# Four layers of a convolution network in float32: the attention heads of the first image's first layer, written as a pinned pipeline over key blocks

## The chip, the cores and the metric

The kernel runs on one core of one Trainium2 chip, in float32 throughout. The metric is the device time of one whole call in microseconds (us), which is the time from the first to the last instruction of all four images. The time before the change is the median of three runs.

## The reference, cut to what matters

Four residual layers are applied to four images of 32 x 32 positions and 384 channels. The change touches only the first layer, and only for the first image. That layer is an attention with six heads of 64 channels, deformed sampling positions, and a bias that is interpolated from a table for each pair of query and key:

```python
q = einsum('bhwc,cd->bhwd', x, w_q) + b_q
# a grouped 3x3 convolution of q, layer norm, gelu and tanh give pos, the sampling positions
xs = _bilinear_sample(xg, pos)
k = (xs @ w_k + b_k).reshape(Bq, n, HEADS, HC)
v = (xs @ w_v + b_v).reshape(Bq, n, HEADS, HC)
attn = einsum('bmhc,bnhc->bhmn', qh, k) * scale
bias = _bilinear_sample(rpe_img, disp)         # disp: from every query to every pos
attn = softmax(attn + bias, axis=-1)
out = einsum('bhmn,bnhc->bmhc', attn, v)
return out @ w_out + b_out                      # x + this goes to layers 1, 2 and 3
```

Here n is 1024, so each head has 1024 queries by 1024 keys. Layers 1 to 3 (a second attention, a box filter and a neighbourhood attention) are not touched.

## The kernel before, in words

Two lanes produce the instructions. The class `Front` computes layer 0 and the class `Trunk` computes layers 1, 2 and 3. Each lane takes its SBUF buffers from its own side: `Front` from the right, `Trunk` from the left (L90, the pools of `scope`, L293 to L298). `Net.layer0` (L257) runs the front of image 0 to its end before anything else is written down. After that `Net.layer3` (L271) writes the trunk of image b and mixes in the fronts of images 1 to 3, so that a front stays a tenth of an image ahead of the trunk (`TRUNK_STEPS`, `FRONT_STEPS`, `LEAD`, L62). So the front of image 0 stands alone, and the trunk of image 0 cannot begin before it, because it reads `x1`, which is that front's result.

Within each engine's queue the framework decides at build time, by its own estimate, which instruction comes next; the order of the program is only a priority. An instruction that is passed to `keep_in_program_order` (called `pin` in the code) is fixed behind everything that was written before it on its engine. Each engine works off its queue in order. A buffer tag with `bufs=k` has k places, and a new tile waits until the last reader of the place is done.

`Front.layer0` (L402) has three stages. `inputs0` (L518) makes the padded queries `qpad`, the sampling positions, the indices `widx` and weights `bias_f` of the bias, then the keys `k0` (L707, in DRAM) and the values `va` (L712). The heads stage (scope "l0b", L416 to L424) runs over 6 heads `h`, 2 halves `q` of 512 queries, and in `head0` (L719) over 8 blocks `j` of 128 keys, which makes 96 blocks in 12 halves. The last stage (L425 to L434) is the output projection.

For one block, `head0` does this. GpSimd gathers a window of the bias table (`win`, L734). ScalarE scales its upper rows into `z` (L746) and VectorE adds the scaled lower rows (L747). ScalarE scales the left columns into `lg` (L751) and VectorE adds the scaled right columns (L752). TensorE multiplies keys by queries (L755), VectorE adds the product to `lg` (L756) and takes the running maximum (L759, L761). After eight blocks the maximum is brought to all partitions: four transposes on TensorE (L768), a reduction on VectorE (`top`, L772), a diagonal on GpSimd (`diag`, L774), a product with ones on TensorE (L776), a copy on ScalarE (`tb`, L780). Only then each of the eight blocks has `tb` subtracted (L787, VectorE), is exponentiated (L788, ScalarE) and goes into two products, with the values and with ones for the row sums (L790). Two copies (L794, L797) and a DMA (L798) save the half. After each pair of heads `over_sums` (L801) loads the row sums through DRAM, takes the reciprocal (L808), sends it through DRAM again (L811, L816) and multiplies `qpad` by it (L821).

In `head0` nothing is pinned. The buffers of the heads stage lie in the place on the right side that `inputs0` used before: 4 places for `win`, 3 for `z`, 13 for `lg`.

## Time and profile before

| what | value |
|---|---|
| median of three runs | 4876.06 us (4868.23 to 4881.34) |
| the profiled execution's own time | 4831.1 us |
| its span from the first to the last instruction | 4829.3 us |
| mean granted TensorE clock | 0.91 of full speed |
| TensorE busy | 4189.8 us, 87% of the span |
| VectorE busy | 3132.9 us, 65% |
| ScalarE busy | 2404.9 us, 50% |
| GpSimd busy | 946.3 us, 20% |

The profile is one execution on the chip. Busy time is the time in which an engine worked on at least one instruction. A group of the profile shows one line of the code on one engine, with the count, the mean duration of one in nanoseconds, and the idle time of the engine just before these instructions with what ended it ("<-"). The table of stretches shows, for each stretch of time, its length, then for each engine the busy us and in brackets the number of instructions, then the granted TensorE clock, the busy share of the DMA engines and their GB/s. Instructions of one engine are pipelined, so the next can start before the one before has ended; a duration is therefore a little longer than the distance between two starts.

In the profiled execution the last instruction of the value projection (L712) of image 0 starts at 221.78 us, the heads stage follows, and its last running maximum ends at 599.7 us.

### The profile page before, as it was taken

What the parts mean: (1) busy time and instruction counts of PE and PEld (TensorE: products, weight loads), DVE (VectorE), ACT (ScalarE), POOL (GpSimd) and SP (SyncE); (2) the same over time, 40 slices, a digit from 0 to 9 for tenths busy, and PEclk for the clock granted to TensorE, in tenths of its full rate; (3) what the DMA queues carried; (4) which work ended last, traced back from release to release, by engine and by line L of the source; (5) the groups of instructions that cost most, each with busy time, mean ns of one, the idle gap of its engine ahead of it and who ended that gap; (6) DMA issues with size and microseconds to landing.
All of it is one profiled execution on the core that took longest, in us unless ns stands there. A gap on an engine that the chain in (4) does not pass through costs nothing.

```text
span 4829.3 us, 46659 instructions
## 1 busy us (share of the span) xinstructions
PE 4189.8 (87%) x15704; PEld 1799.4 (37%) x15704; DVE 3132.9 (65%) x5727; ACT 2404.9 (50%) x3693; POOL 946.3 (20%) x946
## 2 busy tenths in 40 slices
PE   5466678899999989889999989899999998999998
PEld 2222233333333353333333444343333335343444
DVE  3478828676877836577777762767687873454544
ACT  2155414565766513376666532457576641456642
POOL 1533303211212101421211210422121210000000
PEclk7677788999999989899999989799999998899998
DMA  6323244311212143431221224532121213201011
GB/s 118 102 84 92 70 131 144 94 53 38 80 50 73 36 147 105 126 86 50 60 62 54 65 76 113 154 92 56 33 80 42 75 45 114 87 23 33 19 39 40
DMA packets 230927, 366.82 MB, mean 76 GB/s; under 512 B 117475, under 2 KB 164672, under 8 KB 230688
## 3 DMA queue, kind: packets, MB, share of 16 engines
q1 hardware_dynamic: 169672, 197.36, 14.0%
q0 software_dynamic: 39936, 145.53, 10.3%
q10 hardware_dynamic: 21080, 20.96, 1.8%
q8 instruction: 124, 2.03, 0.2%
q14 instruction: 115, 0.94, 0.1%
HBM read 285.84 MB, written 78.21 MB: 75 GB/s over the span
## 4 chain that ended last, share of the span: by engine, by line
PE 35%; ACT 9%; DVE 7%; issue 3%; DMA 2%; POOL 0%; SPq 0%; ACTq 0%; DVEq 0%; POOLq 0%
PE bank L1184 8%; PE big L1154 4%; PE big L376 3%; PE big L1035 3%; PE bank L790 3%; PE bank L390 2%; PE bank L755 2%; PE bank L1128 2%; ACT big L1044 2%; PE bank L1179 2%; DVE e L1193 1%; DVE nmax L1043 1%; ACT e L1162 1%; PE big L1074 1%; PE bank L1472 1%
## 5 line engine op out<-in xcount | busy, mean ns | idle before, releaser
L1193 DVE SCALAR_TENSOR_TENSOR e<-bank,gam,e 128x512 f32<-128x512 f32 x768 | 557.6, 748 | 564.9 <-ACT gn L1192 275.1
L1184 PE MATMUL bank<-sim,sg 128*128 128x512 f32 (+3 forms) x2304 | 870.6, 512 | 2.8 <-DVE e L1193 2.8
L1044 ACT ACTIVATE big<-big,nmax 128x1024 f32<-128x1024 f32 x384 | 418.5, 1090 | 384.5 <-DVE nmax L1043 384.0
L734 POOL DMA_INDIRECT win<-strips,widx x384 | 425.8, 1109 | 887.4 <-DVE z L747 450.3
L1162 ACT ACTIVATE e<-big 128x1024 f32<-128x1024 f32 x384 | 376.8, 1019 | 360.2 <-PE big L1154 355.0
L1184 PEld LDWEIGHTS bank<-sim,sg 128*128 128x128 f32 x2304 | 405.9, 199 | 378.1 <-issue 297.7
L1043 DVE TENSOR_REDUCE nmax<-big 128x1 f32<-128x1024 f32 x384 | 453.1, 1217 | 54.4 <-PE big L1035 53.0
L1154 PE MATMUL big<-qa,ka 64*128 64x512 f32 x1536 | 412.1, 627 | 15.5 <-ACT big L1044 9.4
L1139 POOL TENSOR_SCALAR sg<-sim,gam 128x512 f32<-128x512 f32 x192 | 147.3, 770 | 1416.5 <-PE bank L1184 1126.9
L1035 PE MATMUL big<-k,q 32*128 32x512 f32 x1536 | 357.6, 701 | 74.5 <-ACT e L1162 37.0
L790 PE MATMUL bank<-lg,va 128*64 128x512 f32 x768 | 374.1, 634 | 44.7 <-ACT lg L788 44.6
L755 PE MATMUL bank<-qpad,kz 128*128 128x512 f32 x768 | 375.8, 620 | 22.6 <-DVE e L1193 13.7
L790 PE MATMUL bank<-lg,ones 128*64 128x512 f32 x768 | 373.4, 634 | 0.0
L746 ACT ACTIVATE z<-win,bias_f 128x528 f32<-128x528 f32 x384 | 277.0, 737 | 188.8 <-DVE lg L752 108.6
L752 DVE SCALAR_TENSOR_TENSOR lg<-z,bias_f,lg 128x512 f32<-128x512 f32 x384 | 299.9, 795 | 45.5 <-ACT lg L751 43.9
L747 DVE SCALAR_TENSOR_TENSOR z<-win,bias_f,z 128x528 f32<-128x528 f32 x384 | 291.8, 779 | 38.5 <-ACT z L746 38.1
L652 POOL DMA_INDIRECT gat<-pairs,sidx x192 | 210.8, 1098 | 448.1 <-DVE ix_gt L464 244.5
L751 ACT ACTIVATE lg<-z,bias_f 128x512 f32<-128x512 f32 x384 | 267.5, 719 | 44.1 <-DVE z L747 27.2
L787 DVE TENSOR_TENSOR lg<-lg,tb 128x512 f32<-128x512 f32 x384 | 246.2, 698 | 64.7 <-ACT tb L780 64.7
L756 DVE TENSOR_TENSOR lg<-bank,lg 128x512 f32<-128x512 f32 x384 | 256.3, 683 | 32.0 <-PE bank L755 30.7
L788 ACT ACTIVATE lg<-lg 128x512 f32<-128x512 f32 x384 | 222.4, 629 | 40.2 <-DVE lg L787 39.8
L1154 PEld LDWEIGHTS big<-qa,ka 64*128 64x128 f32 x1536 | 134.7, 188 | 272.0 <-issue 156.8
(262 smaller groups left out, 5812.2 us busy)
## 6 DMA issues: line engine op xcount, KB each, us to landing
pairs<-xn SPq DMA_DIRECT2D x64, 192.0 KB
q<-qd SPq DMA_DIRECT2D x48, 256.0 KB
w<-in_gmat SPq DMA_DIRECT2D x16, 576.0 KB
w<-in_w_off SPq DMA_DIRECT2D x12, 576.0 KB
w<-in_Wqkv SPq DMA_DIRECT2D x12, 576.0 KB
a<-in_x SPq DMA_DIRECT2D x16, 384.0 KB
x<-a ACTq DMA_DIRECT2D x4, 1536.0 KB
k<-a SPq DMA_DIRECT2D x12, 512.0 KB
```

Source lines behind the costliest of these rows:

```text
L734: nc.gpsimd.indirect_dma_start(out=win, out_offset=None, in_=self.strips[:, :], in_offset=bass.IndirectOffsetOnAxis(ap=self.widx[:, q, c : ...
L747: v.scalar_tensor_tensor(z, wv[:, 1 : HH + 1, 0 : HW + 1], sc(0, 1), z, ALU.mult, ALU.add)
L752: v.scalar_tensor_tensor(lg, z[:, :, 1 : HW + 1], sc(0, 0), lg, ALU.mult, ALU.add)
L755: nc.tensor.matmul(ps, kz[:, j * P : (j + 1) * P], both, start=True, stop=True)
L790: nc.tensor.matmul(po[out, :], w, lf, start=j == 0, stop=j == NJ - 1)
L1035: nc.tensor.matmul(ps[r][:, h * 512 : (h + 1) * 512], self.q4[rows, i * P : (i + 1) * P], self.k4[rows, 0:512], start=True, stop=True,)
L1043: v.tensor_reduce(nmax[:, r, i : i + 1], ps[r], AX.X, ALU.max, negate=True)
L1044: nc.scalar.activation(ps[r], ps[r], AF.Exp, bias=nmax[:, r, i : i + 1], accum_out=den[:, r, i : i + 1],)
L1154: nc.tensor.matmul(ps[:, r, :], ka[rows, j * P : (j + 1) * P], qa[rows, cols], start=True, stop=True,)
L1162: nc.scalar.activation(e, ps, AF.Exp)
L1184: nc.tensor.matmul(ps[:, (mid - i0) * P :], sg[:, r, m, :], sim[:, r, m, mid * P : i1 * P], start=m == 0, stop=m == 1,)
L1193: v.scalar_tensor_tensor(e[:, r, :], ps, self.gam[:, 1:2], e[:, r, :], ALU.add, ALU.mult, accum_out=tot[:, r, h : h + 1],)
```

## The change

Only image 0 is changed; images 1 to 3 still use `head0`. The heads of image 0 are now written by a new generator `heads0`. It has one sequence of 96 blocks across all heads and halves, and in each turn `t` it does one step of each phase for different blocks: the window gather for block t+13, the two bias steps on VectorE for blocks t+8 and t+7, the two on ScalarE for t+8 and t+9, the key products for t+2 and t+3 (every second turn, into one two-bank tile), the addition and the running maximum for block t, the subtraction and the exponential for block t-10, the two value products for block t-11. The steps of the maximum follow at the turn of a half, and `divide` does the work of `over_sums` in three steps, 0, 4 and 9 turns after the pair's last block was saved. All compute instructions are pinned; DMAs and gathers are not. The buffers are on the left side, with 8 places for `win`, 5 for `z` and 23 for `lg`. The generator is started inside `inputs0`, ahead of the key and value projections, where it writes turns -9 to -4; the rest follows after `inputs0`. The output projection is moved unchanged into `outputs0`.

```diff
@@ -411,6 +411,17 @@
             self.va = self.wt([P, NJ, C], "va")
             self.f = self.wt([P, 2, 2, NJ * G], "bias_f")
             self.widx = self.wt([P, 2, NJ * G], "widx", 1, I32)
+            if b == 0:
+                self.side = "left"
+                with self.scope("l0f"):
+                    self.side = "right"
+                    self.heads = self.heads0(self.work)
+                    with self.scope("l0a"):
+                        yield from self.inputs0(b)
+                    yield from self.heads
+                yield from self.outputs0(b)
+                return
             with self.scope("l0a"):
                 yield from self.inputs0(b)
             with self.scope("l0b"):
@@ -422,16 +433,20 @@
                         yield from self.head0(h, q)
                     if h % 2:
                         yield from self.over_sums(h // 2)
-            with self.scope("l0c"):
-                w = self.weights("w_out")
-                for ko in range(KC):
-                    rows = slice(ko * P, (ko + 1) * P)
-                    x = self.wt([P, N], "res", 2)
-                    nc.sync.dma_start(x, self.x0[b % 2][rows, :])
-                    ps = self.dense_t(w, self.qpad, ko)
-                    v.scalar_tensor_tensor(x, ps, self.col(C_BOUT, ko), x, ALU.add, ALU.add)
-                    nc.sync.dma_start(self.x1[b % 2][rows, :], x)
-                    yield 6
+            yield from self.outputs0(b)
+    def outputs0(self, b):
+        nc, v = self.nc, self.nc.vector
+        with self.scope("l0c"):
+            w = self.weights("w_out")
+            for ko in range(KC):
+                rows = slice(ko * P, (ko + 1) * P)
+                x = self.wt([P, N], "res", 2)
+                nc.sync.dma_start(x, self.x0[b % 2][rows, :])
+                ps = self.dense_t(w, self.qpad, ko)
+                v.scalar_tensor_tensor(x, ps, self.col(C_BOUT, ko), x, ALU.add, ALU.add)
+                nc.sync.dma_start(self.x1[b % 2][rows, :], x)
+                yield 6
 
     def positions(self, oall):
 
@@ -698,6 +713,9 @@
                 xss[j] = weigh(j, gats.pop(j))
             if j > 0:
                 yield 7
+        if b == 0:
+            next(self.heads)
         va = self.va
         kT = self.wt([P, KC, N], "a12", 2)
         w = self.weights("w_k")
@@ -797,6 +815,199 @@
         nc.scalar.copy(den, po[o0 : o0 + 1, :])
         nc.sync.dma_start(self.den[h][:, q * HN : (q + 1) * HN], den)
         yield 3
+    def heads0(self, work):
+        nc, v, pin = self.nc, self.nc.vector, self.tc.keep_in_program_order
+        f, va = self.f, self.va
+        HH, HN = HW // 2, N // 2
+        NI = HN // P
+        blocks = [(h, q, j) for h in range(G) for q in range(2) for j in range(NJ)]
+        n = len(blocks)
+        AHEAD, SUB, OUT = 8, 10, 11
+        win, z, lg, ps, half, dens, inv = {}, {}, {}, {}, {}, {}, {}
...
+        def divide(step, k):
+            heads = (2 * k, 2 * k + 1)
...
+            if step == 0:
+                dens[k] = tile_of([P, 2, NJ], "dens", 2)
+                for r, h in enumerate(heads):
+                    nc.sync.dma_start(dens[k][:, r, :], by_row(self.den[h]))
+            elif step == 1:
+                pin(v.reciprocal(dens[k], dens[k]))
+                for r, h in enumerate(heads):
+                    nc.sync.dma_start(by_row(self.rden[h]), dens[k][:, r, :])
+                for q in range(2):
+                    inv[q] = tile_of([P, HN], "lg", 23)
+                    for r, h in enumerate(heads):
+                        nc.sync.dma_start(
+                            inv[q][r * GC : (r + 1) * GC],
+                            self.rden[h][0, q * HN : (q + 1) * HN].partition_broadcast(GC),
+                        )
+            else:
+                for q in range(2):
+                    out = queries(2 * k, q)
+                    w = inv[q].rearrange("p (y x) -> p y x", x=HW)
+                    pin(v.tensor_tensor(out, out, w, ALU.mult))
+        def turn(t):
+            i = t + AHEAD
+            if i + 5 < n:
+                h, q, j = blocks[i + 5]
+                win[i + 5] = tile_of([P, (HH + 1) * WROW], "win", 8)
...
+            at = lambda i: blocks[i][2] * G + blocks[i][0]
+            sc = lambda i, axis, side: f[:, side, axis, at(i) : at(i) + 1]
+            if 0 <= i < n:
+                wv = win.pop(i).rearrange("p (r c) -> p r c", c=WROW)
+                pin(v.scalar_tensor_tensor(
+                    z[i], wv[:, 1 : HH + 1, 0 : HW + 1], sc(i, 1, 0), z[i], ALU.mult, ALU.add
+                ))
+            if 0 <= i - 1 < n:
+                zi, lf = z.pop(i - 1), lg[i - 1].rearrange("p (y x) -> p y x", x=HW)
+                pin(v.scalar_tensor_tensor(
+                    lf, zi[:, :, 1 : HW + 1], sc(i - 1, 0, 0), lf, ALU.mult, ALU.add
+                ))
+            if 0 <= i < n:
+                lg[i] = tile_of([P, HN], "lg", 23)
+                pin(nc.scalar.activation(
+                    lg[i].rearrange("p (y x) -> p y x", x=HW),
+                    z[i][:, :, 0:HW],
+                    AF.Copy,
+                    scale=sc(i, 0, 1),
+                ))
+            if 0 <= i + 1 < n:
+                wv = win[i + 1].rearrange("p (r c) -> p r c", c=WROW)
+                z[i + 1] = tile_of([P, HH, HW + 1], "z", 5)
+                pin(nc.scalar.activation(
+                    z[i + 1], wv[:, 0:HH, 0 : HW + 1], AF.Copy, scale=sc(i + 1, 1, 1)
+                ))
+            if t >= -2 and (t + 2) % 16 == 0 and t + 18 < n and t + 2 >= 16:
+                self.load_keys(blocks[t + 18][0])
+            if t >= -2 and t % 2 == 0 and t + 2 < n:
+                big = self.big()
+                for u in range(2):
+                    h, q, j = blocks[t + 2 + u]
+                    ps[t + 2 + u] = big[:, u * 512 : (u + 1) * 512]
+                    pin(nc.tensor.matmul(
+                        ps[t + 2 + u],
+                        self.kz[h % 2][:, j * P : (j + 1) * P],
+                        queries(h, q),
+                        start=True,
+                        stop=True,
+                    ))
+            m = (t - 1) // NJ
+            if t > 0 and t % NJ == 0 and t <= n:
+                top = tile_of([P, NI], "top", 2)
+                pin(v.tensor_reduce(
+                    top, half[m, "t"].rearrange("p (i n) -> p i n", i=NI), AX.X, ALU.max
+                ))
+                diag = tile_of([P, NI, P], "diag", 1)
+                pin(nc.gpsimd.tensor_tensor(
+                    diag, bc(self.ident, 1, NI), bc(top, 2, P), ALU.mult
+                ))
+            if 0 <= t < n:
+                m, j = divmod(t, NJ)
+                pin(v.tensor_tensor(lg[t], ps.pop(t), lg[t], ALU.add))
+                if j == 0:
+                    half[m] = tile_of([P, HN], "rmax", 2)
+                else:
+                    first = lg[t - 1] if j == 1 else half[m]
+                    pin(v.tensor_tensor(half[m], first, lg[t], ALU.max))
+                if j == NJ - 1:
+                    half[m, "t"] = self.bank()
+                    for i in range(NI):
+                        cols = slice(i * P, (i + 1) * P)
+                        pin(nc.tensor.transpose(half[m, "t"][:, cols], half[m][:, cols], self.ident))
+            if t > 1 and t % NJ == 1 and t <= n + 1:
+                m = (t - 2) // NJ
+                half[m, "b"] = tile_of([P, HN], "tb", 2)
+                pin(nc.scalar.copy(half[m, "b"], half[m, "p"]))
+            s = t - SUB
+            if 0 <= s < n:
+                tb = half[s // NJ, "b"]
+                pin(v.tensor_tensor(lg[s], lg[s], tb, ALU.subtract))
+                pin(nc.scalar.activation(lg[s], lg[s], AF.Exp))
+            o = t - OUT
+            if 0 <= o < n:
+                h, q, j = blocks[o]
+                if j == 0:
+                    half[o // NJ, "o"] = self.bank()
+                po = half[o // NJ, "o"]
+                for own, w in ((True, va[:, j, h * GC : (h + 1) * GC]), (False, self.ones[:, 0:GC])):
+                    pin(nc.tensor.matmul(
+                        po[rows(h, own), :], w, lg[o], start=j == 0, stop=j == NJ - 1
+                    ))
+            if t > 0 and t % NJ == 0 and t <= n:
+                m = (t - 1) // NJ
+                half[m, "p"] = self.bank()
+                pin(nc.tensor.matmul(
+                    half[m, "p"], self.ones, diag.rearrange("p i n -> p (i n)"),
+                    start=True, stop=True,
+                ))
+            o = t - OUT - 1
+            if 0 <= o < n and o % NJ == NJ - 1:
+                h, q, j = blocks[o]
+                po, own = half[o // NJ, "o"], rows(h, True)
+                pin(nc.scalar.copy(
+                    queries(h, q)[own], po[own, :].rearrange("p (y x) -> p y x", y=HH)
+                ))
+                o0 = rows(h, False).start
+                den = lg[o][o0 : o0 + 1, :]
+                pin(nc.scalar.copy(den, po[o0 : o0 + 1, :]))
+                nc.sync.dma_start(self.den[h][:, q * HN : (q + 1) * HN], den)
+            o = t - OUT - 2
+            for step, late in enumerate((0, 4, 9)):
+                if o >= late and (o - late) % (4 * NJ) == 4 * NJ - 1:
+                    divide(step, (o - late) // (4 * NJ))
+        for i in range(4):
+            h, q, j = blocks[i]
...
+        for t in range(-AHEAD - 1, -3):
+            turn(t)
+        yield 0
+        self.load_keys(0)
+        self.load_keys(1)
+        for t in range(-3, n + OUT + 12):
+            turn(t)
+        yield 0
 
     def over_sums(self, k):
```

## The prediction

> **What bounds the kernel now.** I read the busy time by slices first, then cut the span at the ends of image 0's front, then looked at VectorE's groups, waits and order of time in the heads stage. From the page's second part:
>
> ```profile
> PE   5466678899999989889999989899999998999998
> DVE  3478828676877836577777762767687873454544
> PEclk7677788999999989899999989799999998899998
> ```
>
> One digit is a fortieth of the span, 121 us. From the seventh slice on TensorE is nearly always busy. The first five slices, image 0's front alone, show TensorE at 4 to 6 tenths, a lower TensorE clock, and VectorE at 7 to 8 tenths from the third to the fifth slice. The table of stretches, cut at the end of the weighing of samples (193.1), the end of L712 (222.3), the last running maximum (599.7) and the end of the last output addition (642.3):
>
> ```profile
> 193.10:222.30 29.20, 29.15 (x77) 15.49 (x78) 8.27 (x11) 0.48 (x1) 0.00 (x0) 0.92 0.28 93
> 222.30:599.70 377.40, 229.26 (x618) 78.66 (x616) 311.52 (x478) 197.04 (x314) 131.30 (x107) 0.77 0.30 87
> 599.70:642.30 42.60, 26.82 (x66) 9.72 (x66) 11.09 (x15) 7.87 (x12) 2.32 (x2) 0.76 0.27 86
> 500.00:520.00 20.00, 7.83 (x15) 2.75 (x13) 20.00 (x31) 11.26 (x17) 10.19 (x9) 0.67 0.39 110
> ```
>
> In the second row VectorE (third pair) works 311.5 of 377.4 us and is idle 65.9; TensorE 229.3, ScalarE 197.0 and GpSimd 131.3 have room. In the last row VectorE is never idle: 31 starts in 20 us, 0.645 us each. Before the stage, in the first row, VectorE works 8.3 of 29.2 us. What ended VectorE's idle time in the heads stage (waiting group, releaser: us in total, times, longest):
>
> ```profile
> DVE dens L808 <- DMA dens<-den: 18.7, 2, 9.6
> DVE lg L756 <- PE bank L755: 11.6, 16, 2.0
> DVE z L747 <- ACT z L746: 11.4, 4, 5.6
> DVE lg L787 <- ACT tb L780: 9.9, 5, 4.0
> DVE qpad L821 <- DMA lg<-rden: 7.7, 2, 4.0
> DVE lg L752 <- ACT lg L751: 4.4, 6, 1.4
> ```
>
> So VectorE's own work bounds this stage, with a sixth of it lost at four kinds of place: the row sums' trips through DRAM (L808, L821), the first products of a half (L756), the wait for the first windows (L747), the maximum's way round the engines (L787). VectorE in order of time (start, duration, idle before in brackets):
>
> ```profile
> 346.08 4.90 DVE L787 TENSOR_TENSOR lg<-lg,tb 128x512 f32<-128x512 f32 x8 [3.90 <-ACT tb L780]
> 360.55 0.25 DVE L808 RECIPROCAL dens<-dens 128x16 f32<-128x16 f32 x1 [9.56 <-DMA dens<-den]
> 360.71 1.32 DVE L752 SCALAR_TENSOR_TENSOR lg<-z,bias_f,lg 128x512 f32<-128x512 f32 x2
> 366.05 0.69 DVE L821 TENSOR_TENSOR qpad<-qpad,lg 128x512 f32<-128x512 f32 x1 [4.01 <-DMA lg<-rden]
> ...
> 549.63 4.90 DVE L787 TENSOR_TENSOR lg<-lg,tb 128x512 f32<-128x512 f32 x8
> 554.45 0.74 DVE L752 SCALAR_TENSOR_TENSOR lg<-z,bias_f,lg 128x512 f32<-128x512 f32 x1
> ```
>
> **What the Trainium skill says.** "TensorE: Matmul & The Clock Gate", section "Architectural detail", calls ScalarE's and VectorE's queues strict FIFO. That fits the row above: the reciprocal held VectorE 9.56 us, so the place of each pinned instruction counts. The same page, "What's actually happening", says that TensorE is throttled to half by default and that activity releases it. The stretches agree: 0.77 in the heads stage, 0.92 in the dense stretch before it. "ScalarE: Activation LUTs", "Table sets", says copy is in every table set, so Copy and Exp may alternate block by block without a table load; in the heads stage the trace shows one load (1283 ns) among 192 copies with a scale and 88 exponentials, though they alternate in bursts.
>
> **The change, part by part.**
>
> *VectorE's work.* No VectorE instruction is added or removed, only moved. Distances between starts when it isn't idle, from rows in order of time: eight L787 take 4.82 us to the next start, 0.60 each; L756 and L761 alternate at 0.60; L747 0.68; L752 0.66. A block costs 0.68 + 0.66 + 3 x 0.60 = 3.14 us. The 20 us without idle time gives 5 x 0.645 = 3.23, because it has GpSimd's diagonal and gathers beside it. I take 3.2 us for a turn.
>
> *The start.* The windows' gathers no longer wait for `inputs0`'s buffers (before, the first waited for L712 until 222.5 and its scaling came at 227.2). Turns -9 to -4 put 5 L747 and 4 L752, 6.0 us, and their ScalarE steps behind the last weighing at 193.1, where VectorE is idle 20.9 of 29.2 us. Queued behind them is the key projection's L706 (first at 199.2); if all nine stood ahead of it, as a chain (L747 0.77, then L751 0.72, L746 0.74 and hand-overs, 2.23 us from one L747 to the next in the trace at 227.9 and 230.2), they would end near 206 and cost up to 7 us of the projections. I count 2. Turns -3 to -1 come after L712 and run at this chain: 3 x 2.23 = 6.7, so turn 0 begins at 229.0 (231.0 with the 2).
>
> *Turns 0 to 95, up to the last maximum.* VectorE has 88 L747-like, 89 L752-like, 96 additions, 84 maxima, 86 subtractions, 11 reductions, 2 reciprocals and 4 multiplications by the reciprocal: 460. By the distances this is 59.8 + 58.7 + 266 x 0.60 (159.6) + 6.6 + 2.8 = 287.5 us; by 0.645 each, 296.7. I take 292.
>
> *The waits that go.* Row sums: `divide` gives the first DMA trips 4 turns (12.8 us) and the second 5 (16 us). In the trace the second trip took 360.55 to 366.05, 5.5 us, and the first wait was 9.6 us at most: both are covered, 26.4 us of idle time gone. Key products are issued 2 turns (6.4 us) ahead of their addition; two cost TensorE 1.72 us at full clock (the starts of L755 are 0.43 apart and a product takes two). The windows are gathered 4 turns, 12.8 us, ahead of use; they land after 3.9 us, 8.4 at the longest. `tb` is ready before the subtraction of its half's first block if its chain takes less than the two turns from reduction to use, 6.4 us plus 1.2; from the end of the last maximum at 599.7 it took 5.4 us to 605.06.
>
> *The waits that may come.* In its pinned order VectorE stands at the reduction while TensorE's four transposes wait for the last maximum. A subtraction and two bias steps (1.94 us) lie between them; the trip took 0.8. TensorE stands at the product with ones until the diagonal is done, and behind it the next products, which have two turns in hand. ScalarE has 0.62 + 0.64 + 0.55 us per block plus 1.75 per half, 2.0 of a 3.2 us turn; the exponential stands behind the copy of `tb`, and the next bias steps behind the exponential. SP keeps the key loads 16 turns ahead of use; before and after them only the small row-sum DMAs stand, nothing on their path. GpSimd has 1.24 + 1.15/8 = 1.4 us per turn. None of these is shown in this order by the trace, so I bound their sum: 0 if every cover holds, 36 us if each of 12 halves loses 3 us. I take 10.
>
> *After the last maximum* the chain is the same as before (subtractions, exponentials, products, sums through DRAM, projection: 42.6 us), so nothing changes. The trunk's clearing of its own buffers on the left side (10 instructions near 0.95 us and two of 0.3, on GpSimd, before at 18.8 to 38) now waits for the heads' buffers. GpSimd is idle 38.7 us before the `qpad` clearing at 641, and the first reader comes by DMA at 751: cover, cost 0; 10 us at most if that cover were gone.
>
> *Sum.* The last maximum ends at 231 + 292 + 10 = 533 instead of 599.7: 66.7 us earlier. Everything later hangs on `x1`, TensorE is full from there, so it moves by the same amount; I take off 1.7 for changed order later, 65. Against the profiled execution's 4831.1 us this gives 4766; that execution is 45 us (0.9%) below the median of 4876.06, so on the median I subtract the same 65: **4811 us**.
>
> **The rivals.** *(A) Part of the gain is taken by new waits* (chance 0.22). For it: TensorE's clock. At half clock a block costs two products at 0.855 us for the keys (1.71), 1.71 for the pair with values and ones (starts 0.855 apart at 581 to 583), and a third of a us for its share of transposes and the product with ones (L776 at 1141 ns each shows the half clock): 3.75 us, more than 3.2. If half the turns ran so, the mean is 3.48, 27 us more: gain near 38, 4838 us. Against it: at full clock TensorE needs 1.9 us per turn, a lag of 0.55 us per turn is absorbed by the two turns in hand for some ten turns, and a TensorE that is always busy gets its clock back, as the dense stretch shows.
>
> *(B) No gain* (0.05): the pipeline runs at half clock throughout, 96 x 3.75 = 360 us from 229 on, 589 instead of 599.7: 4866 us. This is also where the change would land if the pinned order did not overlap halves at all.
>
> *(C) Slower* (0.05): half clock, and in addition the chain of `tb` at every half. Its product with ones (2.1 us) then stands behind key and value products (up to 5.1 us), and with diagonal (1.15) and copy (0.58) the chain takes 9 us where about 6 are covered; ScalarE stands at the copy, so bias steps and VectorE stand too. 12 x 3 = 36 us on top of (B): 4876 + 25 = 4901 us. It decides from a mean turn of (599.7 - 229)/96 = 3.86 us on.
>
> *(D) More gain* (0.05): VectorE at 3.1 us per turn and no new wait, 75 to 85 us, 4796 us.
>
> **How the numbers follow.** The forecast, a gain of 50 to 75 us, has 0.63. The range leaves out (C), most of (B) and the tails of (A) and (D): 4793 to 4848 us. A difference of 0.3% (15 us) is about what a measurement of this kernel can tell from no change. Faster by more: forecast, (A) and (D), 0.90; within: (B), 0.05; slower: (C), 0.05.
>
> **What would show it.** In the profile after, the last maximum of image 0 near 533 us; from turn 10 on VectorE idle under 0.2 us per block, starts 3.2 us apart for one kind; no wait at the reciprocal; the first L747-like step before 200 us; the stretch from the last maximum to the last output addition near 42.6 us; the rest from there 4187 us, as now. Wrong would be: TensorE near 100% busy with a clock near 0.5 in the stage, long waits of VectorE for key products or the transposes, or a rest longer than 4187 us by more than 10.

## The result and the profile after

The changed kernel takes 4803.94 us (median of four runs, 4803.23 to 4812.72) against 4872.15 us of the kernel before in the same series; the ratio is 0.9865, with a 95% interval from 0.9848 to 0.9881. That is 68 us less; 65 were forecast, with 4811 us for the time and 4793 to 4848 for the range.

The page after, second part, slices of 120 us:

```profile
PE   5477798999999898899999989799999998999988
DVE  3599655777877727577778744667686873455544
PEclk8689897999999987999999989799999998899998
```

The third and fourth slice, image 0's heads, now show VectorE at 9 tenths (7 and 8 before) and TensorE's clock at 8 and 9 (7 and 7). The table of stretches, cut at the first bias step (193.28; before, at the end of the weighing, 193.1), at 222.3 as before (here the last value addition starts at 219.41, so this row holds the first 2 us of the heads too), at the last running maximum and at the last output addition:

```profile
193.28:222.30 29.02, 29.02 (x79) 14.85 (x77) 15.81 (x23) 8.12 (x12) 9.15 (x9) 0.97 0.66 209
222.30:532.70 310.40, 223.16 (x591) 65.67 (x590) 304.55 (x464) 191.70 (x296) 111.31 (x93) 0.88 0.32 95
532.70:574.40 41.70, 30.68 (x89) 10.84 (x87) 13.69 (x18) 9.06 (x16) 12.69 (x20) 0.88 0.20 63
574.40:4802.00 4227.60, 3841.99 (x14560) 1662.27 (x14560) 2726.63 (x5084) 2172.03 (x3312) 745.44 (x751) 0.93 0.24 73
```

Second row: VectorE works 304.6 of 310.4 us. Its idle time is 5.9 us instead of 65.9, while its work is nearly the same (304.6 and 311.5). First row: up to 222.3 it does twice what it did (15.8 instead of 8.3 us). The waits of VectorE in the stage that are longer than 0.15 us, of which six kinds were shown before, are now these:

```profile
DVE z L885 <- ACT z L904: 2.4, 4, 0.8
DVE lg L954 <- ACT tb L949: 1.3, 1, 1.3
```

One turn in VectorE's order of time, and the last maximum of the stage (start, duration):

```profile
414.57 0.76 DVE L885 SCALAR_TENSOR_TENSOR z<-win,bias_f,z 128x528 f32<-128x528 f32 x1
415.25 0.74 DVE L890 SCALAR_TENSOR_TENSOR lg<-z,bias_f,lg 128x512 f32<-128x512 f32 x1
415.91 0.68 DVE L935 TENSOR_TENSOR lg<-big,lg 128x512 f32<-128x512 f32 x1
416.63 0.69 DVE L940 TENSOR_TENSOR rmax<-rmax,lg 128x512 f32<-128x512 f32 x1
417.24 0.68 DVE L954 TENSOR_TENSOR lg<-lg,tb 128x512 f32<-128x512 f32 x1
417.84 0.76 DVE L885 SCALAR_TENSOR_TENSOR z<-win,bias_f,z 128x528 f32<-128x528 f32 x1
...
531.97 0.69 DVE L940 TENSOR_TENSOR rmax<-rmax,lg 128x512 f32<-128x512 f32 x1
```

A turn takes 417.84 - 414.57 = 3.27 us. Four of its five distances are those of the kernel before (0.68, 0.66, 0.61, 0.60); one is not: the maximum starts 0.72 us after the addition, not 0.60. The last maximum ends at 532.66, 67.0 us earlier than before.

The row for the rest, 4227.6 us, is 40.6 us longer than in the profiled execution before (4187.0). In that part the two programs have the same instructions in the same order on every engine, apart from one table load. The prediction had named a rest longer by more than 10 us as a sign of being wrong, and the first two experiments ask where these 41 us belong. The medians above lie 31 to 37 us higher, for both kernels, than those of the experiments. On which chip that first series ran is not on record, so a run is only compared with the kernel before on its own chip, and stages are compared by the end of the last running maximum (M) and of the last output addition (O).

M also holds what the stages ahead took in that execution. Two traces of the kernel before have M at 599.6 and 597.1 us. So each trace has a second mark, G, the start of the first gather of samples for the keys and values (L667, or L652 of the kernel before). Ahead of it every run has the same instructions in the same order on each engine, apart from GpSimd's clearing of the trunk's buffers (18 instructions). From G to M the kernel before takes 477.9 and 477.7 us in its two traces, the changed kernel 413.0 and 413.5.

### The profile page after: what moved, and what is told of

It reads as the page before. It is cut to its first block, busy times and chain, and to the rows that moved or that the text cites. A ratio compares the mean times of both kernels' runs of the same rounds, so it can differ in the third digit from the quotient of the medians.

```text
span 4802.0 us, 46610 instructions
## 1 busy us (share of the span) xinstructions
PE 4201.4 (87%) x15704; PEld 1793.1 (37%) x15704; DVE 3136.5 (65%) x5727; ACT 2411.3 (50%) x3693; POOL 942.6 (20%) x946
## 5 line engine op out<-in xcount | busy, mean ns | idle before, releaser
L752 POOL DMA_INDIRECT win<-strips,widx x288 | 308.1, 1070 | 629.2 <-DVE z L765 328.1
L1365 PE MATMUL big<-qa,ka 64*128 64x512 f32 x1536 | 414.1, 630 | 14.8 <-ACT big L1255 8.8
L667 POOL DMA_INDIRECT gat<-pairs,sidx x192 | 210.1, 1094 | 500.6 <-DVE ix_gt L479 401.7
L773 PE MATMUL bank<-qpad,kz 128*128 128x512 f32 x576 | 283.0, 617 | 15.0 <-DVE e L1404 15.0
L808 PE MATMUL bank<-lg,va 128*64 128x512 f32 x576 | 265.0, 602 | 16.3 <-ACT lg L806 16.2
L808 PE MATMUL bank<-lg,ones 128*64 128x512 f32 x576 | 264.3, 602 | 0.0
L770 DVE SCALAR_TENSOR_TENSOR lg<-z,bias_f,lg 128x512 f32<-128x512 f32 x288 | 227.9, 803 | 40.1 <-ACT lg L769 38.6
L764 ACT ACTIVATE z<-win,bias_f 128x528 f32<-128x528 f32 x288 | 207.1, 739 | 63.3 <-DVE lg L770 39.2
L765 DVE SCALAR_TENSOR_TENSOR z<-win,bias_f,z 128x528 f32<-128x528 f32 x288 | 216.2, 769 | 27.0 <-DMA win<-strips,widx 16.6
L1339 PE MATMUL bank<-e,vs 128*32 128x512 f32 x1536 | 210.9, 605 | 2.1 <-DVE vs L1333 2.1
L769 ACT ACTIVATE lg<-z,bias_f 128x512 f32<-128x512 f32 x288 | 201.4, 720 | 19.1 <-PE bank L808 10.7
L376 PE MATMUL big<-xh,w 128*128 128x512 f32 x432 | 199.3, 619 | 12.2 <-ACT big L1255 10.8
```

Source lines behind the costliest of these rows:

```text
L376: nc.tensor.matmul(ps[:, h * 512 : (h + 1) * 512], w[:, ki, lo + ko * P : lo + (ko + 1) * P], mov, start=ki == 0, stop=ki == KC - 1,)
L752: nc.gpsimd.indirect_dma_start(out=win, out_offset=None, in_=self.strips[:, :], in_offset=bass.IndirectOffsetOnAxis(ap=self.widx[:, q, c : ...
L773: nc.tensor.matmul(ps, kz[:, j * P : (j + 1) * P], both, start=True, stop=True)
L808: nc.tensor.matmul(po[out, :], w, lf, start=j == 0, stop=j == NJ - 1)
L1339: nc.tensor.matmul(av[r0 : r0 + HD1, :], vs[:, r, :], es[h][:, r, :], start=j == 0, stop=j == NJ - 1,)
L1365: nc.tensor.matmul(ps[:, r, :], ka[rows, j * P : (j + 1) * P], qa[rows, cols], start=True, stop=True,)
```

## The experiments

The times are medians, the ratio is to the kernel before on the same chip (4835.0 to 4838.3 us there), G, M and O are from each run's trace.

| run | time | ratio, 95% interval | G | M | O | M - G |
|---|---|---|---|---|---|---|
| before, again | 4837.15 | 1.0002 (0.9994 to 1.0010) | 119.4 | 597.1 | 639.8 | 477.7 |
| changed, again | 4772.52 | 0.9862 (0.9839 to 0.9885) | 119.7 | 533.2 | 575.1 | 413.5 |
| changed, no pins | 4756.26 | 0.9841 (0.9814 to 0.9867) | 119.5 | 513.0 | 555.0 | 393.5 |
| changed, late start | 4781.82 | 0.9881 (0.9857 to 0.9906) | 123.6 | 547.6 | 589.0 | 424.0 |
| changed, row sums at once | 4786.75 | 0.9898 (0.9879 to 0.9917) | 120.2 | 548.0 | 589.0 | 427.8 |
| before, left side | 4815.26 | 0.9952 (0.9933 to 0.9970) | 121.9 | 585.4 | 628.0 | 463.5 |
| before, row sums late | 4815.93 | 0.9944 (0.9922 to 0.9966) | 121.4 | 578.8 | 621.6 | 457.4 |
| changed, maximum last | 4763.02 | 0.9850 (0.9834 to 0.9867) | 120.6 | 530.7 | 572.3 | 410.1 |
| changed, maximum last, long start | 4754.03 | 0.9836 (0.9820 to 0.9853) | 120.9 | 521.3 | 562.5 | 400.4 |
| changed, no maximum | 4679.04 | 0.9670 (0.9654 to 0.9686) | 120.4 | none | 482.0 | none |
| no pins, half the additions on TensorE | 4717.99 | 0.9745 (0.9727 to 0.9763) | 120.7 | 482.0 | 522.2 | 361.3 |
| no pins, two thirds on TensorE | 4714.25 | 0.9743 (0.9722 to 0.9763) | 119.5 | 479.1 | 519.5 | 359.6 |

### Both kernels again, on one chip

> The kernel before, once more and with a profile of its own. The instructions after the front of image 0 stand in the same order on every engine in both kernels, yet in the two profiled executions they take 4187 us before and 4228 us after. Theory: the heads stage alone makes the difference of the medians (68 us) and the 41 us lie between two executions, not between two programs; then this run's part after the front takes about 4228 us and its time is near 4872 us. Rival: the change makes the rest 41 us longer; then this run's rest takes about 4187 us and its time is near 4831 us.

> The changed kernel once more, on the same chip as the kernel before. Theory: 67 us less than the kernel before (4800 to 4810 us), the last running maximum of image 0 at 533 us, the rest as long as in the run of the kernel before within 5 us. Rival (the change lengthens the rest): the rest 41 us longer than in the run of the kernel before, total only 27 us less.

Measured: 4837.15 and 4772.52 us. The rows from the last output addition to the end, of the kernel before and then of the changed one, in their new traces:

```profile
639.80:4826.30 4186.50, 3826.28 (x14560) 1656.11 (x14560) 2725.18 (x5084) 2169.88 (x3311) 748.39 (x751) 0.93 0.25 73
```

```profile
575.10:4769.30 4194.20, 3835.86 (x14560) 1660.46 (x14560) 2726.24 (x5085) 2171.42 (x3312) 744.76 (x751) 0.93 0.25 73
```

The rest takes 4186.5 and 4194.2 us. So the 41 us are no property of the change; over the twelve traces here the rest lies between 4179.5 and 4200.2 us without order. Taken alone, the first run has the numbers that its expectation gave to the rival (4187 us of rest); the second decides against it. The two rests differ by 7.7 us, a little more than the 5 that were allowed, but the traced execution of the kernel before is the fastest of its 20 runs (4828.14 us), 9 us below their median. The 4872 and 4800 to 4810 us that were expected were the level of the first series. From G to M the stage is 64.2 us shorter (477.7 to 413.5), by M alone 63.9 (597.1 to 533.2), the median is 62.5 us lower (4835.0 of the kernel before beside it, to 4772.52). Why the rest took 4228 us in the one trace of the first series is open.

### No pins

```diff
-        nc, v, pin = self.nc, self.nc.vector, self.tc.keep_in_program_order
+        nc, v, pin = self.nc, self.nc.vector, lambda ins: ins
```

> The changed kernel with no instruction pinned: the framework orders the heads as it estimates, with the pipelined program as its priority. Theory (the pinned order keeps VectorE busy): VectorE waits again at some of the places where it waited before; the last running maximum ends 5 to 40 us later than 533, the time rises by as much. Rival (the places on the other side of SBUF and the early start do it, the pins nothing): 533 us, no change of time. Second rival (the framework does it better): earlier than 528 us.

M = 513.0: the second rival. The pinned order as it was written costs 20 us up to M; by the medians it is 16 us (4772.52 to 4756.26), with intervals of the ratios that overlap. VectorE during the projections, first without pins, then in the changed kernel, from its first bias step to the start of the last value addition:

```profile
190.10:221.80 31.70, 28.84 (x76) 15.24 (x77) 30.30 (x44) 22.79 (x34) 23.81 (x22) 0.87 0.88 279
```

```profile
193.30:219.90 26.60, 26.60 (x72) 13.93 (x71) 14.00 (x20) 6.83 (x11) 8.27 (x8) 0.95 0.66 214
```

Without pins VectorE (third pair) is busy 30.3 of 31.7 us there, with them 14.0 of 26.6. Up to 222 us the free order has done 17 first and 15 second bias steps, the pinned one 6 and 5; that is 11 x 0.68 + 10 x 0.66 = 14.1 us of work which no longer stands in the stage. In the free order 78 of the 84 maxima don't follow an addition directly, at 0.12 us each (9.4 us; the run with the maximum last tests this price). It waits 6.2 us at the reduction, where the changed kernel waits 3.9 us for ScalarE. The three make 14.1 + 9.4 - 2.3 = 21.2 us, against 20.0 from G to M. My theory, that pins keep VectorE busy, is wrong: the pipelined program does it without them.

### Late start

```diff
-        if b == 0:
-            next(self.heads)
         va = self.va
...
             v.tensor_tensor(va[:, j, :], ps, bv, ALU.add)
+        if b == 0:
+            next(self.heads)
```

> The changed kernel with the first turns (-9 to -4) written after the key and value projections instead of ahead of them. Theory: this undoes the start alone; gathers are still free to go early, but the nine VectorE steps and their chain (5 turns of 2.2 us) come after the value projection's last addition: the last running maximum ends 9 to 14 us later than 533, total 4812 to 4818 us. Rival (the start is worth nothing, the first windows are not on the path): within 3 us of 533.

M = 547.6, 14.4 us later. But this execution was 3.9 us late already at G (123.6 against 119.7), ahead of anything that the edit touches. From G to M it is 10.5 us more, by the medians 9.3. The start is on the path and worth the lower part of what was expected.

### The row sums: three steps in one turn, and the old kernel with late row sums

```diff
-            for step, late in enumerate((0, 4, 9)):
+            for step, late in enumerate((0, 0, 0)):
```

> The changed kernel with the three steps of the row sums written in one turn, without the 4 and 5 turns between them. Theory: the reciprocal then holds VectorE for the first trip through DRAM (about 9.6 us) and the multiplication for the second (about 5 us), at two pairs of heads inside the stage: last running maximum near 561 us, 26 to 30 us more in all. Rival (the trips are hidden by other work anyway): within 5 us of 533.

M = 548.0: 14.8 us later, 14.3 from G on, half of what was expected. Two of VectorE's waits:

```profile
DVE qpad L865 <- DMA lg<-rden: 11.5, 4, 5.3
DVE dens L851 <- DMA dens<-den: 4.3, 2, 2.5
```

For the second trip VectorE waits 5.7 us for each pair of heads (11.5 for two); before it was 3.9 (7.7 for two), with two bias steps in between. The first one costs 2.5 at most, not 9.6: the row sums are saved one turn ahead and the reciprocal stands at the end of its turn, so that most of this trip lies under five VectorE instructions.

```diff
                     for q in range(2):
                         yield from self.head0(h, q)
+                        if b == 0 and q == 0 and h in (2, 4):
+                            yield from self.over_sums(h // 2 - 1)
-                    if h % 2:
+                    if h % 2 and (b > 0 or h == 5):
                         yield from self.over_sums(h // 2)
```

> The kernel before with one part of the change: for image 0 the work on the row sums of a pair of heads is written after the first half of the next head instead of ahead of it. Theory: the 26 us in which VectorE waited for the two trips through DRAM go, and nothing else: last running maximum near 571 instead of 597 us. Rival (seen when the three steps were put in one turn: only 15 us lost there): the trips cost 15 us, 582 us. Second rival (in an order that the framework chooses they are hoisted back): 597 us.

M = 578.8: 18.3 us of the 26, and 20.3 from G on, since this execution was 2 us late at G. Its longest waits in the stage:

```profile
DVE lg L758 <- PE bank L757: 21.3, 25, 2.3
DVE lg L789 <- ACT tb L782: 10.3, 6, 3.9
DVE z L749 <- ACT z L748: 6.7, 2, 5.5
DVE lg L754 <- ACT lg L753: 6.4, 11, 1.4
```

The trips through DRAM are gone from the list, but the wait for the key products rose from 11.3 to 21.3 us. A wait that is taken away in the old order is partly taken over by the next one.

### The old program with the buffers on the left side

```diff
+            if b == 0:
+                self.side = "left"
             with self.scope("l0b"):
+                self.side = "right"
...
-            win = self.wt([P, (HH + 1) * WROW], "win", 4)
+            win = self.wt([P, (HH + 1) * WROW], "win", 8 if self.wide else 4)
```

`z` and `lg` likewise have 5 and 23 places for image 0.

> The kernel before with one part of the change: the heads' buffers of image 0 are on the left side, with 8, 5 and 23 places instead of 4, 3 and 13; the program of the heads is the old one, unpinned, and nothing starts inside the first stage. Theory (the order of the program does most): it gains from the start and some overlap of halves, the row sums still hold VectorE (26 us): last running maximum at 555 to 580 us instead of 597. Rival (places alone): 540 us or earlier.

M = 585.4, 11.7 us earlier and 14.2 from G on, less than the 17 to 42 of the theory; the median is 21.5 us lower. The rival (540 us or earlier) falls. The first bias step starts at 192.5 here, so the early start comes with the places alone, but the row sums still hold VectorE and the wait for key products doubles (from 11.3 us):

```profile
DVE lg L760 <- PE bank L759: 24.3, 16, 7.2
DVE dens L812 <- DMA dens<-den: 20.2, 2, 10.2
DVE lg L791 <- ACT tb L784: 12.3, 6, 3.9
DVE qpad L825 <- DMA lg<-rden: 8.6, 2, 4.7
```

### The maximum last, and a longer start

```diff
-                if j == 0:
-                    half[m] = tile_of([P, HN], "rmax", 2)
...
                 pin(v.tensor_tensor(lg[s], lg[s], tb, ALU.subtract))
                 pin(nc.scalar.activation(lg[s], lg[s], AF.Exp))
+            if 0 <= t < n:
+                m, j = divmod(t, NJ)
+                if j == 0:
+                    half[m] = tile_of([P, HN], "rmax", 2)
...
```

> The changed kernel with the subtraction (block t-10) written before the running maximum (block t) in each turn; nothing else. In the changed kernel the maximum starts 0.72 us after the addition whose result it reads, every other VectorE instruction 0.60 to 0.68 us after the one ahead of it. Theory: VectorE waits for a result that the instruction just ahead of it writes, 0.12 us each time; with another instruction between, 84 of these waits go, the last running maximum ends near 523 instead of 533 us, the time falls by 10 us. Rival: the 0.12 us belong to the maximum (two operands in SBUF, one of them written in place) or to the change between PSUM and SBUF operands; then nothing changes.

A turn of it:

```profile
316.18 0.76 DVE L885 SCALAR_TENSOR_TENSOR z<-win,bias_f,z 128x528 f32<-128x528 f32 x1
316.86 0.74 DVE L890 SCALAR_TENSOR_TENSOR lg<-z,bias_f,lg 128x512 f32<-128x512 f32 x1
317.52 0.68 DVE L935 TENSOR_TENSOR lg<-big,lg 128x512 f32<-128x512 f32 x1
318.12 0.68 DVE L944 TENSOR_TENSOR lg<-lg,tb 128x512 f32<-128x512 f32 x1
318.72 0.69 DVE L952 TENSOR_TENSOR rmax<-rmax,lg 128x512 f32<-128x512 f32 x1
319.32 0.76 DVE L885 SCALAR_TENSOR_TENSOR z<-win,bias_f,z 128x528 f32<-128x528 f32 x1
```

The same maximum with the same operands now starts 0.60 us after what is ahead of it, and the turn is 3.14 us. So the 0.12 us belong to reading what the instruction just ahead has written; the rival that put them down to the maximum itself falls. So does the one of a change between PSUM and SBUF operands, since here the subtraction, with operands in SBUF, follows the addition, which reads PSUM, at 0.60. The first 8 maxima, which have no subtraction ahead of them yet, still start 0.72 us after their additions. But M is only 2.5 us earlier, 3.4 from G on, not 10. The 76 waits that are gone make 9.1 us. Against them the waits of the bias step for ScalarE rose from 2.6 to 5.2 us and those of the subtraction for `tb` from 1.3 to 2.9, since a faster turn leaves ScalarE less time; 1.1 us of new waits came at the reduction and the addition, and M itself is one subtraction (0.60) later in its turn: 5.9 us in all. (By the medians, each against the kernel before on its own chip, the gain would be 11 us; the intervals overlap.) A faster turn ran into the next limit.

```diff
-        AHEAD, SUB, OUT = 8, 10, 11
+        AHEAD, SUB, OUT = 10, 10, 11
...
-        for t in range(-AHEAD - 1, -3):
+        for t in range(-AHEAD - 1, 0):
```

The key products of turn -2 stay behind the key loads, and `lg` has 25 places.

> As the one before, and turns -11 to -1 (bias steps of ten blocks, two more places for lg) are written ahead of the key and value projections instead of turns -9 to -4 (five blocks). Theory: the 20 us by which the version without pins is earlier come from the start, where VectorE has room during the projections, and from the 0.12 us waits; then this one reaches the version without pins: last running maximum at 512 to 516 us, 18 us below the changed kernel. Rival: the pinned bias steps stand in front of the key projection's VectorE work and delay it, so the gain is eaten: 523 us or later, last addition of the value projection later than 222 us.

M = 521.3: 9.4 us from the longer start (9.7 from G on). 5 more bias steps of each kind stand under the projections (6.7 us), and the three chain turns between the projections and turn 0 are gone. The rival falls. M doesn't reach the version without pins (513.0). The 0.12 us waits are not the reason, as only 8 of the 84 maxima still stand behind their additions. But up to 222 us it has done 11 first and 10 second bias steps, the free order 17 and 15: 6 x 0.68 + 5 x 0.66 = 7.4 us, and 6.9 are missing from G on. By the medians the two are not told apart: ratios of 0.9836 with pins and 0.9841 without.

### No maximum

```diff
-                else:
-                    first = lg[t - 1] if j == 1 else half[m]
-                    pin(v.tensor_tensor(half[m], first, lg[t], ALU.max))
...
-                pin(v.tensor_tensor(lg[s], lg[s], tb, ALU.subtract))
```

The reduction, the diagonal, the transposes, the product with ones and the copy to `tb` are taken out with them.

> The changed kernel without the running maximum, its way to all partitions and the subtraction, for image 0 only; the exponential is taken of the plain logits, so the softmax has no protection against overflow. It leaves VectorE 3 of 5 instructions per block (2.0 us) and takes work from every engine. Theory (VectorE's own work sets the turn of 3.27 us): the turn falls to what binds next, the chain bias step on VectorE, two on ScalarE, next bias step, 2.2 us; first to last addition of a block about 95 x 2.2 = 209 us instead of 300, total 90 to 105 us below the changed kernel. Rival (TensorE at a low clock or the gathers set the turn): first to last addition above 270 us.

The time falls by 93.5 us against the changed kernel (the two were on different chips, whose kernels before agree within 2.2 us). From the first to the last addition it takes 214 us (209 expected). A half of eight blocks takes 18.6 us instead of 26.7, 2.3 us per turn, and what binds is the chain that was expected:

```profile
DVE z L885 <- ACT z L904: 26.4, 86, 1.2
DVE lg L925 <- PE big L915: 5.2, 3, 2.5
```

So neither the gathers nor TensorE (165 of 200 us busy between 228 and 428 us, at a clock of 0.95) sets the changed kernel's turn; VectorE does. TensorE has less to do in this version, but what is left of its work and all gathers fit into the shorter turn.

### Additions on TensorE

```diff
                         start=True,
-                        stop=True,
+                        stop=not u % 2 == 1,
                     ))
+                    if u % 2 == 1:
+                        pin(nc.tensor.matmul(
+                            ps[t + 2 + u], self.ident, lg[t + 2 + u], start=False, stop=True
+                        ))
...
-                pin(v.tensor_tensor(lg[t], ps.pop(t), lg[t], ALU.add))
+                if not t % 2 == 1:
+                    pin(v.tensor_tensor(lg[t], ps.pop(t), lg[t], ALU.add))
...
+            c = t + 1
+            if 0 <= c < n and c % 2 == 1:
+                pin(nc.scalar.copy(lg[c], ps.pop(c)))
```

Here `pin` does nothing, as in the version without pins.

> The changed kernel without pins, and for every second block the addition of the bias to the key product is done by TensorE (a second product of the identity with lg, accumulated in the same bank) and a copy on ScalarE instead of on VectorE: 48 VectorE additions (0.60 us each) less, 48 products (0.86 us at full clock) and 48 copies (about 0.5 us) more. Theory (VectorE sets the stage, TensorE has 1.9 us per turn at full clock and ScalarE 2.0): the stage ends 20 to 29 us earlier than without pins alone, output addition at 526 to 535 instead of 555 us. Rival (TensorE and ScalarE have no room left at the ends of the halves): within 8 us of 555, or later.

O = 522.2, 32.8 us earlier than without pins, somewhat more than the 20 to 29 expected; why it is more was not tried. One row of the stage, with TensorE's clock at 1.00 and VectorE without idle time:

```profile
300.00:400.00 100.00, 88.92 (x258) 25.88 (x258) 100.00 (x153) 81.04 (x129) 51.66 (x39) 1.00 0.42 118
```

In the next version only each third addition stays with VectorE:

```diff
-                        stop=not u % 2 == 1,
+                        stop=(t + 2 + u) % 3 == 0,
...
-                    if u % 2 == 1:
+                    if (t + 2 + u) % 3:
...
-                if not t % 2 == 1:
+                if t % 3 == 0:
...
-            if 0 <= c < n and c % 2 == 1:
+            if 0 <= c < n and c % 3:
```

> As the version without pins and with every second addition on TensorE, but with two of three. VectorE loses 16 more additions (9.6 us), TensorE gets 16 products more (0.86 us each at full clock) and ScalarE 16 copies. In the version with every second one VectorE had no idle time to speak of and TensorE was busy for 73 to 76 of 78 to 80 us. Theory A (VectorE still sets the stage): output addition at 511 to 515 instead of 522 us. Theory B (both are full, TensorE becomes the bound): 520 us or later, with VectorE waiting for key products.

O = 519.5, 2.7 us better, of which 1.2 were there at G: theory B. TensorE is busy 96.4 of 100 us in the same stretch. VectorE waits 6.3 us for the transposes, and 0.8 for the key products that B had named. The two versions are equal within their intervals. Both beat both kernels: 4714.25 us is 0.9743 of the kernel before.

## Why the prediction was right, and where its terms were off

**The bound.** VectorE's own work set the stage, as said: its idle time fell from 65.9 to 5.9 us, and taking two of its five instructions and each half's reduction away shortened the turn by 1 us. This is shown.

**The sum.** Forecast for the last maximum was 533 us, measured 532.7; the tail after it 42.6, measured 41.7; the gain 65, measured 68 (62.5 in the pair on one chip). From G to M the gain was 64.9 us in the first pair of traces and 64.2 in the second. The agreement of the first number is partly luck, because two terms were off and cancel:

- *The start.* Turn 0 was put at 231.0; its first instruction started at 226.44, 4.6 us earlier. The projections were not delayed by 2 us. The last value addition started at 219.4 instead of 221.8; that is no merit of the change but a matter of the executions, since G was at 119.6 instead of 121.7, and in the second trace of the kernel before this addition starts at 219.35. The chain of the three first turns was right (219.88 to 226.44, 2.19 us each; 2.23 forecast).
- *The turns.* 292 us of work and 10 of new waits were forecast, 302; it took 532.7 - 226.4 = 306.3. The 10 us of waits for other engines were 2.4 + 1.3 = 3.7 us, at two of the places that I named. The larger term is 84 x 0.12 = 10.1 us between addition and maximum, which the sum had at nothing: I had taken this distance at 0.60 from a stretch of the kernel before where another block's addition stood between the two. The forecast allowance came out near the size of a cost that it didn't mean; that is luck.

**The waits that go.** Those for the row sums, the first products and the left columns left the list. Those for the first windows (11.4 us) and for `tb` (9.9) shrank to 2.4 and 1.3. What each was worth is another matter: 26.4 us of idle at the row sums were 14.3 us of time from G to M when put back, 20.3 when taken from the old kernel alone. For the start the prediction gave no number of its own; undoing it cost 10.5 us. The remaining 64.2 - 10.5 - 14.3 = 39.4 us are left for the overlap of halves and the products issued ahead; this is a difference, no run had them alone.

**The pins.** I argued only whether their order would hold. As written they cost 20 us up to M against the same program in free order; the prediction has no term for it. It is the places that they fix, and not pinning as such: with the maximum last and a longer start the pinned version has the same median as the free one within the intervals.

**The rivals.** A, B and C rested on a lower TensorE clock. It rose from 0.77 to 0.88, and TensorE was busy 223 of 310 us. I had given them 0.32 together; the trace of before did say that a dense stretch has a high clock (0.92), and this deserved more weight. The cover for the clearing of the trunk's buffers held: GpSimd has 20 instructions in a tail that is no longer than before, and the rest of the program didn't grow on the same chip by more than its scatter.

## What to carry to other kernels

Where one engine has work for four fifths of a stage and waits for the others at fixed places, write the blocks as one sequence across the loop's borders and lay the long trips several turns ahead; count the gain as the engine's idle time (here 60 us less of it, for a stage 64 us shorter), but not wait by wait, since a wait that goes is partly taken over by the next. Start such a pipeline under the stage ahead of it, as far as buffers allow, and try the order without pins too: here it showed how many more steps had room there. Then look for the next engine with room: here it was TensorE, which took half of one of VectorE's five steps.

## What the runs showed of the hardware that was not expected

A VectorE instruction that reads what the one just ahead of it has written starts 0.72 us after it; with another one between, it starts 0.60 us after that one (128x512, float32, durations 0.68; all 84 maxima of the changed kernel, median 0.719, against 76 in the version with the maximum last, median 0.599). The maximum carries a wait on a semaphore of VectorE's own in these traces, so 0.12 us is the price of such a wait for the instruction just ahead; how a reader without it would start, no run here shows. The Trainium skill, "VectorE: DVE Perf Modes", section "The DRAIN you can't avoid", says that the next instruction doesn't start until the pipe is empty, and in the same paragraph that one which isn't held starts earlier. The traces agree with the second: independent instructions start 0.08 us before the end of the one ahead, and the one that reads its result starts after it (0.72 against 0.68).

GpSimd's diagonal lengthens a VectorE instruction with two SBUF operands that runs beside it, once in each half: 1.33 instead of 0.68 us at 410.04 in the changed kernel. "SBUF — State Buffer", section "Who interferes with whom", in the Trainium skill says that such instructions contend with GpSimd's reads; the trace agrees, with 0.47 to 0.66 us each, 6.8 us in eleven halves. The later it starts beside the diagonal, the less it is lengthened: by 0.65 us when 0.27 us after it (410.04 and 409.77), by 0.47 when 0.43 us after it (490.12 and 489.69).
